# Moving three small pieces of work in a two-layer graph kernel: the x loads, one operand load, and the row degrees

## The chip, the cores and the metric

The kernel runs on one core of a Trainium2 chip. The metric is device time in microseconds (us) of one execution. Engines are named as in the profile: PE is TensorE, DVE is VectorE, ACT is ScalarE, POOL is GpSimd, SP is SyncE, which here only issues DMA transfers.

## The reference: what is computed

The inputs are features x (4096 x 512), an adjacency matrix adj (4096 x 4096, about 0.8% of it non-zero, all entries at or above zero) and a weight matrix W (512 x 512), all fp32.

```python
mask = incidence_m > 0
head = mask / maximum(sqrt(sum(mask * mask, axis=-1)), EPS)
inc = incidence_m + head                      # incidence_m is adj
edge_fea = inc @ cur                          # cur is x
edge_degree = sum(inc, axis=-1)
x = layernorm(x + edge_fea / edge_degree)     # layer 0
A2 = adj + eye
dscale = diagonal(A2) ** -0.5
y = relu((dscale[:, None] * A2 * dscale[None, :]) @ (A2 @ x @ W.T))
x = layernorm(x + y)                          # layer 1
```

The degree of a row is the sum of inc over that row. Since head puts 1/sqrt(count) on each of the count positive entries, the degree also equals the plain row sum of adj plus sqrt(count).

## The kernel before, in words

**Layer 0** multiplies inc (4096 x 4096) by x with one level of a seven-product scheme (Strassen-Winograd): rows and columns are halved, so a block row j (of 16) stands for rows j and j+16 of 128. A block row is cut into four chunks n = 4j + c, each with four inner steps kk of 128. Per kk, `multiply1` issues seven fp32 matmuls into seven PSUM banks; the profile shows each as two instructions. The right operands lie ready in SBUF in `slots[kk]` (seven 256-wide operands, each with two more columns, so W = 258). The two extra columns of B11, B21 and T1 hold ones, so three of the seven matmuls are 258 wide and their column 256 gives the row degree. Block row 0 is done earlier by `multiply_plain`, with four matmuls per kk: first the upper row (h = 0), then the lower (h = 1).

**Where inc comes from.** For every chunk DVE computes raw sums (which POOL sends to DRAM for layer 1), the masks times the row scale (`to_inc`), and the scheme's sums (`add_up`). `prepare1(n + 1)` is written one chunk ahead of `multiply1(n)`. The row scale 1/sqrt(count) of block row j comes from ACT: natural-order tiles `nat` of adj (128 x 512, five buffers, 16 tiles per block row) are loaded on the SP queue; `count(times)` takes each tile, runs Sign in place with a running sum into `cnt` (L377, recorded on L332), and then issues the load of a later tile (L378). `spread(j, 0)` adds the counts on DVE (L384) and takes the square root on ACT (L336). For block rows 1 and 2 the scale then goes through a diagonal matrix `d` on DVE (L393) and a matmul on PE (L408); for later rows through DRAM.

**The start.** SP issues four half chunks of adj (L556), then the loads of x (L315, L316), the other four half chunks, the rest of x, and five `nat` loads. ACT takes signs of the first halves, PE sums them (L343) with some idle products that keep it running (L348), DVE makes the first masks, and the first `multiply_plain` begins. `count(16)` (L594) is written before the last quarter of the upper row, `spread(1, 0)` (L609) after the first quarter of the lower row, and `spread(1, 2)`, with PE's L408, after the second.

**Order.** Every engine takes its instructions in the order in which the program writes them. So what stands behind a waiting instruction on the same engine or on the SP queue waits too. After each block row `combine` empties the seven banks: ACT copies q1 and q5 (L503, L507), DVE adds; PE's next block row needs q1's bank first. These ACT copies stand behind the counts of chunk c = 3. With `deg` (L505, L513) `combine` also collects the degree, and `layer0` divides by it.

**Layer 1** has 224 steps (k, s, p, kk) of seven 512-wide fp32 matmuls. Per step SP loads an operand of adj (`load_up_to`, L217 and others), and every two steps a group of right operands `tr` (`load_b`, L250, three buffers). Group 3 (steps 6 and 7) reads what `operands` leaves for block row 15; that is written at step 1, by POOL. `load_b_up_to` is called at every odd step, at its end (L1026).

Of the kernel before, what the change touches and what calls it, by code (L numbers as in the profile page):

```python
# [8 lines left out]
F32 = mybir.dt.float32  # L9
BF16 = mybir.dt.bfloat16  # L10
AF = mybir.ActivationFunctionType
ALU = mybir.AluOpType

P = 128
# [12 lines left out]
def tile_adj_resnorm_d2(  # L27
# [270 lines left out]
    nc.gpsimd.memset(ones_b, 1.0)  # L298
    ones_f = w1_pool.tile([P, P], F32, name="ones_f", bufs=1)
    nc.gpsimd.memset(ones_f, 1.0)  # L300
    chunks, sums, slots, counts, scale, natural = {}, {}, {}, {}, {}, {}
    xr = {}

    mask = w1_pool.tile([P, 2, CW], F32, name="mask", bufs=1)
# [33 lines left out]
    def count_half(h, c, ps):  # L338

        m = w1_pool.tile([P, 2, CW], F32, name="sr", bufs=2).bitcast(BF16)[:, :, 0:CW]  # L340
        signs(m, chunks[c][:, 2 * h:2 * h + 2, :])
        for z in range(2):
            nc.tensor.matmul(ps, ones_b, m[:, z, :], start=(c + z == 0), stop=(c == NC - 1 and z == 1))  # L343

    def idle_products(times):

# [23 lines left out]
    def count(times):  # L370
        for _ in range(times):
            if not waiting:
                return
            (j, h, t), nat = waiting.pop(0)
            if j not in counts:
                counts[j] = w1_pool.tile([P, 2, NT], F32, name="cnt")
            signs(nat, nat, counts[j][:, h, t:t + 1])  # L377
            load_natural()  # L378

    def spread(j, part):  # L380

        if part == 0:
            n = w1_pool.tile([P, 2], F32, name="n", bufs=2)
            nc.vector.tensor_reduce(n, counts.pop(j), axis=mybir.AxisListType.X, op=ALU.add)  # L384
            to_scale(n, n)
            scale[j] = n
        elif part == 1:
            n = scale.pop(j)
            nc.vector.tensor_scalar(n, n, EPS, None, op0=ALU.max)
            nc.vector.reciprocal(n, n)  # L390
            d = w1_pool.tile([P, 2, P], F32, name="d", bufs=1)
            for h in range(2):
                nc.vector.tensor_scalar(d[:, h, :], ident, n[:, h:h + 1], None, op0=ALU.mult)  # L393
            scale[j] = d
        elif part == 3:

            n = scale.pop(j)
            nc.vector.tensor_scalar(n, n, EPS, None, op0=ALU.max)
            nc.vector.reciprocal(n, n)
            row = dram.tile([P, 2], F32, name=f"sc{j}")  # L400
            nc.gpsimd.dma_start(out=row, in_=n)
            s = w1_pool.tile([P, P, 2], F32, name="sc")
            nc.gpsimd.dma_start(out=s.rearrange("p i h -> p (i h)"), in_=row.rearrange("i h -> (i h)").partition_broadcast(P))
            scale[j] = s.rearrange("p i h -> p h i")
        else:
            d = scale.pop(j)
            ps = spare()
            nc.tensor.matmul(ps[:, 0:2 * P], ones_f, d.rearrange("p h i -> p (h i)"), start=True, stop=True)  # L408
            scale[j] = w1_pool.tile([P, 2, P], F32, name="sc")
            nc.scalar.copy(scale[j].rearrange("p h i -> p (h i)"), ps[:, 0:2 * P])  # L410
# [47 lines left out]
    def multiply1(n, acc, then=None):  # L458
        c = n % NC
        a, s = chunks.pop(n), sums.pop(n)  # L460
        for i in range(CK):
            kk = c * CK + i
            b = slots[kk]
            cols = slice(i * P, (i + 1) * P)
            if then is not None and i == CK - 1:
                then()
            for m, (left, right, w) in enumerate((
                (a[:, A11, cols], B11, W), (a[:, A12, cols], B21, W), (s[:, S2, cols], T2, H),
                (s[:, S1, cols], T1, W), (s[:, S3, cols], T3, H), (s[:, S4, cols], B22, H),
                (a[:, A22, cols], T4, H),  # L470
            )):
                nc.tensor.matmul(acc[m][:, 0:w], left, b[:, right, 0:w], start=(kk == 0), stop=(kk == NP - 1))  # L472

    def multiply_plain(h, c, acc, then={}):

# [12 lines left out]
    def take(h, acc):  # L488

        y = row_tile("z", 2)  # L490
        nc.scalar.copy(y[:, 0:H], acc[0][:, 0:H])
        nc.scalar.copy(y[:, H:D], acc[1][:, 0:H])
        nc.scalar.copy(deg0[:, h:h + 1], acc[0][:, H:H + 1])
        return y

    def combine(acc):

        q1, q2, q6, q5, q7, q3, q4 = acc
        top, low = row_tile("z", 2), row_tile("z", 2)
        p1, p5 = row_tile("p1", 1)[:, 0:W], row_tile("p5", 1)[:, 0:W]  # L500
        u2, u3 = row_tile("u2", 1)[:, 0:H], row_tile("u3", 1)[:, 0:H]
        deg = small.tile([P, 2], F32, name="deg", bufs=2)
        nc.scalar.copy(p1, q1[:, 0:W])  # L503
        nc.vector.tensor_add(top[:, 0:H], q2[:, 0:H], p1[:, 0:H])
        nc.vector.tensor_add(deg[:, 0:1], q2[:, H:H + 1], p1[:, H:H + 1])  # L505
        nc.vector.tensor_add(u2, q6[:, 0:H], p1[:, 0:H])
        nc.scalar.copy(p5, q5[:, 0:W])  # L507
        nc.vector.tensor_add(u3, q7[:, 0:H], u2)
        nc.vector.tensor_add(u2, u2, p5[:, 0:H])
        nc.vector.tensor_add(top[:, H:D], q3[:, 0:H], u2)  # L510
        nc.vector.tensor_sub(low[:, 0:H], q4[:, 0:H], u3)
        nc.vector.scalar_tensor_tensor(low[:, H:D], u3, -1.0, p5[:, 0:H], op0=ALU.mult, op1=ALU.subtract)
        nc.vector.tensor_copy(deg[:, 1:2], p5[:, H:H + 1])  # L513
        return top, low, deg

    def load_rows(j):
        for h in range(2):
# [3 lines left out]

    def layer0(j, C):

        rd = small.tile([P, 2], F32, name="rd", bufs=2)
        nc.vector.reciprocal(rd, C[2])
        stats = []
        for h in range(2):
            y = C[h]
            nc.vector.scalar_tensor_tensor(y, y, rd[:, h:h + 1], xr.pop(h), op0=ALU.mult, op1=ALU.add)
            stats.append(statistics([y]))  # L530
        for h in range(2):
            normalise(C[h], *stats[h])
            nc.gpsimd.dma_start(out=x1_rows[j + h * NP], in_=C[h])

    def operands(j, C):

        top, low, _ = C
        t = row_tile("t", 1, (P, 4, H))
        outer_sums(t, top[:, 0:H], top[:, H:D], low[:, 0:H], low[:, H:D])
        nc.gpsimd.dma_start(out=in_outer(2, j, slice(B11, B11 + 1)), in_=top[:, 0:H].unsqueeze(1))  # L540
        nc.gpsimd.dma_start(out=in_outer(2, j, slice(B21, B22 + 1)), in_=split(low))
        nc.gpsimd.dma_start(out=in_outer(2, j, slice(T1, T4 + 1)), in_=t)
# [7 lines left out]
            work.tile([P, 4, CW], F32, tag="s", name="s")  # L550
    inc11 = work.tile([P, 4, CW], F32, tag="s", name="s")
    scale[0] = w1_pool.tile([P, 2, P], F32, name="sc")
    deg0 = small.tile([P, 2], F32, name="deg", bufs=2)

    def load_half(h, c):
        nc.sync.dma_start(out=chunks[c][:, 2 * h:2 * h + 2, :], in_=adj_q[0, c][:, 2 * h:2 * h + 2, :])  # L556
# [5 lines left out]
    nc.gpsimd.memset(feats[-1][:, 1, T2, 0:H], 1.0)  # L562
    idle = feats[-1][:, 1, T2, 0:H].bitcast(BF16)
    for c in range(NC):
        count_half(0, c, ps)
        idle_products((0, 3, 0, 8)[c])
    for kk in range(10):
        load_x(kk)
    for c in range(NC):
# [2 lines left out]
        load_x(kk)  # L572
    for s in feats:
        nc.gpsimd.memset(s[:, :, B11:B21 + 1, H:W], 1.0)
        nc.gpsimd.memset(s[:, :, T1, H:W], 1.0)
    for _ in range(5):
        load_natural()
    top, low = [bank(0), bank(1)], [bank(6), bank(5)]
# [45 lines left out]
    prepare1(NC)  # L624
    build_last(4)
    multiply_plain(1, 3, low)
    C = top, take(1, low), deg0
    load_rows(0)

    for n in range(NC, NP * NC):  # L630
        j, c = divmod(n, NC)
        if c == 0:
            if j > 1:
                C = combine(acc)
            acc = [bank(m) for m in range(7)]
        if n + 2 >= NP * NC:
            load_up_to(n + 2 - NP * NC)
        else:
            load_chunk(n + 2)
        scales = j < NP - 1 and c == (2 if j == 1 else 1)  # L640
        if scales:
            spread(j + 1, 0)
        if n + 1 < NP * NC:
            prepare1(n + 1, between=(lambda: spread(j + 1, 1 if j == 1 else 3)) if scales else None)
        else:
            prepare(0)
        if n == NC:
            for g in range(5, NP // 2):
                build_last(g)
        multiply1(n, acc, (lambda: spread(j + 1, 2)) if scales and j == 1 else None)  # L650
        count(((6, 6, 4, 6) if j == 1 else (6, 0, 4, 6))[c])
        if j == 1 and c == 1:
            nc.vector.tensor_scalar(dscale, dscale, 1.0, None, op0=ALU.add)
            nc.scalar.activation(dscale, dscale, AF.Sqrt)
            nc.vector.reciprocal(dscale, dscale)
            nc.gpsimd.tensor_scalar(nscale, dscale, -1.0, None, op0=ALU.mult)
        if c == 1:
            layer0(j - 1, C)
        elif c == 2:
            operands(j - 1, C)  # L660
        if c == 3:
            load_rows(j)
# [330 lines left out]
    for n, (k, s, p, kk) in enumerate(steps):  # L993
# [28 lines left out]
                nc.gpsimd.dma_start(out=wt[:, op], in_=parts[f, o])  # L1022
        elif n == 4:
            outer_sums(wt[:, T1:T4 + 1], wt[:, B11], wt[:, T4], wt[:, B21], wt[:, B22])
        if n % 2 == 1:
            load_b_up_to(n // 2 + 3)  # L1026
        for item in items:
            take_up(item)
# [69 lines left out]
```

## Time and profile before

| | |
|---|---|
| median of three runs (lowest to highest) | 2285.16 us (2283.39 to 2285.18) |
| the profiled execution's own time | 2284.03 us |
| its span in the trace | 2282.1 us |
| PE busy | 2255.1 us, 99% of the span |
| DVE, ACT, POOL busy | 1854.4, 417.3, 383.3 us |
| DMA | 555.80 MB, mean 244 GB/s |

The span is what the trace covers; the own time is 1.9 us more. The table of busy time tells which engine is full over the whole; what a change in one place is worth has to be read from the waits and the timeline of that place.

### The profile page before, as it was taken

The numbers are of one execution on the slowest core, as the hardware profiler recorded it, in microseconds if no ns is written. First come the engines' busy times: TensorE is split into PE (matmuls) and PEld (weight loads), VectorE is DVE, ScalarE is ACT, GpSimd is POOL, SyncE is SP. The second block draws the span as 40 slices with busy tenths as digits, with TensorE's granted clock in tenths as the row PEclk, the third lists the DMA queues.
The fourth block names the chain that finished last, engine by engine and source line by source line (L and its number), as shares of the span: only waits on it lengthen the run. The fifth ranks groups of instructions, "written<-read, shape, count | busy, mean of one in ns | idle before, by whom it ended". The sixth has DMA issues, their size and how long they took to land.

```text
span 2282.1 us, 22004 instructions
## 1 busy us (share of the span) xinstructions
PE 2255.1 (99%) x7359; PEld 1380.3 (60%) x7359; DVE 1854.4 (81%) x2619; ACT 417.3 (18%) x991; POOL 383.3 (17%) x548
## 2 busy tenths in 40 slices
PE   8999999999999999999999999999999999999997
PEld 6888888888888844444555444555544444444443
DVE  6988988988988777788876778887666788776788
ACT  4333223332232000000222100122110011100013
POOL 0111112211111110001333300232320000100013
PEclk9999999999999999999999999999999999999999
DMA  9788777878777576575767857576785676766573
GB/s 330 274 287 262 260 233 270 272 262 270 238 240 239 187 266 259 198 283 184 270 240 227 262 209 271 191 283 261 209 256 218 220 258 241 253 238 227 209 269 117
DMA packets 155936, 555.80 MB, mean 244 GB/s; under 512 B 17920, under 2 KB 32272, under 8 KB 117424
## 3 DMA queue, kind: packets, MB, share of 16 engines
q1 hardware_dynamic: 114624, 417.38, 51.6%
q0 software_dynamic: 41200, 137.03, 18.2%
q8 instruction: 58, 0.95, 0.2%
q14 instruction: 54, 0.44, 0.1%
HBM read 434.78 MB, written 119.55 MB: 243 GB/s over the span
## 4 chain that ended last, share of the span: by engine, by line
PE 89%; DVE 5%; DMA 3%; ACT 2%; issue 1%; POOL 0%; SPq 0%; DVEq 0%; ACTq 0%
PE q L278 55%; PE q L472 27%; PE q L766 3%; PE q L485 2%; DMA nat<-adj 2%; DVE s L167 1%; PE q L908 1%; PE q L844 1%; DVE s L169 0%; ACT z L816 0%; ACT nat L332 0%; DVE a L442 0%; DVE mask L435 0%; ACT t L816 0%; DVE ts L257 0%
## 5 line engine op out<-in xcount | busy, mean ns | idle before, releaser
L278 PE MATMUL q<-s,ts 128*128 128x512 f32 x1326 | 612.2, 592 | 0.1
L472 PE MATMUL q<-b,s 128*128 128x256 f32 (+1 forms) x1920 | 454.4, 379 | 0.0
L278 PEld LDWEIGHTS q<-s,ts 128*128 128x128 f32 x1326 | 251.6, 190 | 299.1 <-issue 268.3
L167 DVE TENSOR_TENSOR s<-a 128x1024 f32<-128x1024 f32 x236 | 290.2, 1230 | 161.4 <-PE q L278 131.3
L472 PEld LDWEIGHTS q<-b,s 128*128 128x128 f32 x1920 | 363.1, 189 | 53.1 <-DVE z L510 0.5
L472 PE MATMUL q<-b,a 128*128 128x258 f32 (+1 forms) x1440 | 352.5, 380 | 0.7 <-ACT p L503 0.6
L278 PE MATMUL q<-a,tr 128*128 128x512 f32 x692 | 329.4, 592 | 1.8 <-DMA a<-adj_r 1.8
L472 PEld LDWEIGHTS q<-b,a 128*128 128x128 f32 x1440 | 272.5, 189 | 40.9 <-ACT p L503 1.5
L278 PE MATMUL q<-s,tr 128*128 128x512 f32 x442 | 225.7, 592 | 0.0
L278 PEld LDWEIGHTS q<-a,tr 128*128 128x128 f32 x692 | 129.5, 190 | 145.1 <-issue 138.9
L332 ACT ACTIVATE nat<-nat,tiny 128x512 f32<-128x512 f32 x240 | 170.9, 714 | 235.9 <-DMA nat<-adj 235.7
L278 PE MATMUL q<-a,ts 128*128 128x512 f32 x346 | 176.8, 592 | 0.0
L169 DVE TENSOR_TENSOR s<-a,s 128x512 f32<-128x512 f32 x236 | 167.7, 711 | 8.1
L170 DVE TENSOR_TENSOR s<-a,s 128x512 f32<-128x512 f32 x236 | 167.3, 709 | 8.0
L442 DVE TENSOR_TENSOR a<-a,mask 128x1024 f32<-128x1024 f32 x123 | 150.7, 1225 | 6.6 <-DVE mask L435 0.5
L435 DVE SCALAR_TENSOR_TENSOR mask<-a,sc 128x1024 f32<-128x1024 f32 (+2 forms) x129 | 154.1, 1196 | 2.1
L278 PEld LDWEIGHTS q<-s,tr 128*128 128x128 f32 x442 | 84.0, 190 | 92.1 <-issue 84.6
L684 ACT COPY p<-q 128x512 f32<-128x512 f32 x27 | 15.6, 577 | 631.5 <-PE q L278 631.5
L278 PEld LDWEIGHTS q<-a,ts 128*128 128x128 f32 x346 | 65.7, 190 | 83.0 <-issue 76.1
L425 POOL DMA_DIRECT2D oa<-sr x64 | 57.7, 902 | 283.8 <-DVE sr L416 181.6
L873 POOL DMA_DIRECT2D out<-o x24 | 13.1, 547 | 507.8 <-ACT o L162 507.8
L278 PE MATMUL q<-r,tr 128*128 128x512 f32 x192 | 92.7, 593 | 0.0
(193 smaller groups left out, 2129.4 us busy)
## 6 DMA issues: line engine op xcount, KB each, us to landing
a<-adj_r SPq DMA_DIRECT2D x112, 1024.0 KB, 6.6
a<-oa SPq DMA_DIRECT2D x80, 1024.0 KB, 5.3
nat<-adj SPq DMA_DIRECT2D x240, 256.0 KB, 7.4
a<-adj_q SPq DMA_DIRECT2D x60, 1024.0 KB, 6.2
tr<-ob SPq DMA_DIRECT2D x112, 512.0 KB, 4.0
oa<-sr POOLq DMA_DIRECT2D x64, 512.0 KB, 7.2
oa<-r POOLq DMA_DIRECT2D x32, 1024.0 KB, 9.2
y<-x POOLq DMA_DIRECT2D x64, 256.0 KB, 7.2
```

What stands on the lines that cost most here:

```text
L167: nc.vector.tensor_add(s[:, S3:S1 + 1, :], a[:, A11:A22 + 1, :], a[:, A21, :].unsqueeze(1).to_broadcast([P, 2, w]))
L169: nc.vector.tensor_add(s[:, S2, :], a[:, A11, :], s[:, S1, :])
L170: nc.vector.tensor_add(s[:, S4, :], a[:, A12, :], s[:, S2, :])
L278: nc.tensor.matmul(acc[m], left, right, start=(kk == 0), stop=(kk == NQ - 1))
L332: nc.scalar.activation(y, a, AF.Sign, bias=tiny, scale=2.0 ** 64, accum_out=accum)
L425: nc.gpsimd.dma_start(out=dst, in_=sr.rearrange("p m (k i) -> p (m k) i", i=P))
L435: nc.vector.scalar_tensor_tensor(m, v, 0.0, s.unsqueeze(1).to_broadcast(list(v.shape)), op0=ALU.is_gt, op1=ALU.mult)
L442: nc.vector.tensor_add(z, z, y)
L472: nc.tensor.matmul(acc[m][:, 0:w], left, b[:, right, 0:w], start=(kk == 0), stop=(kk == NP - 1))
L485: nc.tensor.matmul(y[:, 0:w], left, slots[kk][:, op, 0:w], start=(kk == 0 and left is k1), stop=(kk == NP - 1 and left is k2))
L766: nc.tensor.matmul(ps, left[:, e, :], wt[:, right, e, :], start=(e == 0), stop=(e == 1))
L844: nc.tensor.transpose(ps[:, at + i * P:at + (i + 1) * P], C_of[3][h][d // 2][:, 2 * r + d % 2, cols], ident)
```

## The change

Four edits, in this order in time:

1. POOL copies one element of the first sign tile into slot 0 of x, which the first x load then overwrites. So that load, and everything behind it on the SP queue, is issued after ACT has finished the first sign tile.
2. For each `nat` tile ACT first runs a Copy in place with a running sum into a new tile `tot` (L379 of the changed kernel), then the Sign as before. DVE adds these sums per block row and adds sqrt(count), which is the degree. The extra columns go out of `multiply1`, `combine` has no degree work, and POOL no longer writes ones into T1. Block row 0 keeps the 258-wide products.
3. The counts per chunk change from 6, 0, 4, 6 to 5, 4, 5, 2 (block row 1: from 6, 6, 4, 6 to 6, 6, 5, 6); `count(16)` and `count(4)` at the start stay as they are.
4. In layer 1, the call of `load_b_up_to` at step 1 is skipped; step 3 loads groups 3 and 4.

```diff
             if j not in counts:
                 counts[j] = w1_pool.tile([P, 2, NT], F32, name="cnt")
+                totals[j] = w1_pool.tile([P, 2, NT], F32, name="tot")
+            nc.scalar.activation(nat, nat, AF.Copy, accum_out=totals[j][:, h, t:t + 1])
             signs(nat, nat, counts[j][:, h, t:t + 1])
             load_natural()
...
             to_scale(n, n)
+            deg = degrees[j] = w1_pool.tile([P, 2], F32, name="deg", bufs=3)
+            nc.vector.tensor_reduce(deg, totals.pop(j), axis=mybir.AxisListType.X, op=ALU.add)
+            nc.vector.tensor_add(deg, deg, n)
             scale[j] = n
...
-                nc.tensor.matmul(acc[m][:, 0:w], left, b[:, right, 0:w], start=(kk == 0), stop=(kk == NP - 1))
+                nc.tensor.matmul(acc[m][:, 0:H], left, b[:, right, 0:H], start=(kk == 0), stop=(kk == NP - 1))
...
-        nc.vector.tensor_add(deg[:, 0:1], q2[:, H:H + 1], p1[:, H:H + 1])
...
-        nc.vector.tensor_copy(deg[:, 1:2], p5[:, H:H + 1])
...
-        nc.vector.reciprocal(rd, C[2])
+        nc.vector.reciprocal(rd, degrees.pop(j))
...
     for c in range(NC):
-        count_half(0, c, ps)
+        m = count_half(0, c, ps)
+        first_signs = m if c == 0 else first_signs
         idle_products((0, 3, 0, 8)[c])
+    nc.gpsimd.tensor_copy(out=slots[0][:, B11, 0:1], in_=first_signs[:, 0, 0:1])
     for kk in range(10):
         load_x(kk)
...
-        nc.gpsimd.memset(s[:, :, T1, H:W], 1.0)
...
-        count(((6, 6, 4, 6) if j == 1 else (6, 0, 4, 6))[c])
+        count(((6, 6, 5, 6) if j == 1 else (5, 4, 5, 2))[c])
...
-        if n % 2 == 1:
+        if n % 2 == 1 and n > 1:
             load_b_up_to(n // 2 + 3)
```

More of the change, by code (lines that the diff above doesn't have):

```diff
@@ L300, in tile_adj_resnorm_d2 @@
     nc.gpsimd.memset(ones_f, 1.0)
-    chunks, sums, slots, counts, scale, natural = {}, {}, {}, {}, {}, {}
+    chunks, sums, slots, counts, totals, degrees, scale = {}, {}, {}, {}, {}, {}, {}
     xr = {}
@@ L343, in count_half @@
             nc.tensor.matmul(ps, ones_b, m[:, z, :], start=(c + z == 0), stop=(c == NC - 1 and z == 1))
+        return m
     def idle_products(times):
@@ L466, in multiply1 @@
                 then()
[L467 to L470, printed above, removed]
+            for m, (left, right) in enumerate((
+                (a[:, A11, cols], B11), (a[:, A12, cols], B21), (s[:, S2, cols], T2), (s[:, S1, cols], T1),
+                (s[:, S3, cols], T3), (s[:, S4, cols], B22), (a[:, A22, cols], T4),
             )):
-                nc.tensor.matmul(acc[m][:, 0:w], left, b[:, right, 0:w], start=(kk == 0), stop=(kk == NP - 1))
+                nc.tensor.matmul(acc[m][:, 0:H], left, b[:, right, 0:H], start=(kk == 0), stop=(kk == NP - 1))
     def multiply_plain(h, c, acc, then={}):
@@ L492, in take @@
         nc.scalar.copy(y[:, H:D], acc[1][:, 0:H])
-        nc.scalar.copy(deg0[:, h:h + 1], acc[0][:, H:H + 1])
+        nc.scalar.copy(degrees[0][:, h:h + 1], acc[0][:, H:H + 1])
         return y
@@ L499, in combine @@
         top, low = row_tile("z", 2), row_tile("z", 2)
[L500 to L504, printed above, removed]
-        nc.vector.tensor_add(deg[:, 0:1], q2[:, H:H + 1], p1[:, H:H + 1])
-        nc.vector.tensor_add(u2, q6[:, 0:H], p1[:, 0:H])
-        nc.scalar.copy(p5, q5[:, 0:W])
+        p1, p5, u2, u3 = (row_tile(t, 1)[:, 0:H] for t in ("p1", "p5", "u2", "u3"))
+        nc.scalar.copy(p1, q1[:, 0:H])
+        nc.vector.tensor_add(top[:, 0:H], q2[:, 0:H], p1)
+        nc.vector.tensor_add(u2, q6[:, 0:H], p1)
+        nc.scalar.copy(p5, q5[:, 0:H])
         nc.vector.tensor_add(u3, q7[:, 0:H], u2)
-        nc.vector.tensor_add(u2, u2, p5[:, 0:H])
+        nc.vector.tensor_add(u2, u2, p5)
         nc.vector.tensor_add(top[:, H:D], q3[:, 0:H], u2)
         nc.vector.tensor_sub(low[:, 0:H], q4[:, 0:H], u3)
-        nc.vector.scalar_tensor_tensor(low[:, H:D], u3, -1.0, p5[:, 0:H], op0=ALU.mult, op1=ALU.subtract)
-        nc.vector.tensor_copy(deg[:, 1:2], p5[:, H:H + 1])
-        return top, low, deg
+        nc.vector.scalar_tensor_tensor(low[:, H:D], u3, -1.0, p5, op0=ALU.mult, op1=ALU.subtract)
+        return top, low
     def load_rows(j):
@@ L535, in operands @@
     def operands(j, C):
-        top, low, _ = C
+        top, low = C
         t = row_tile("t", 1, (P, 4, H))
@@ L552, in tile_adj_resnorm_d2 @@
     scale[0] = w1_pool.tile([P, 2, P], F32, name="sc")
-    deg0 = small.tile([P, 2], F32, name="deg", bufs=2)
+    degrees[0] = w1_pool.tile([P, 2], F32, name="deg", bufs=3)
     def load_half(h, c):
@@ L626, in tile_adj_resnorm_d2 @@
     multiply_plain(1, 3, low)
-    C = top, take(1, low), deg0
+    C = top, take(1, low)
     load_rows(0)
```

## The prediction

> **What bounds the kernel now.** I read the table of busy time first, then who PE waited for.
>
> ```profile
> PE 2255.1 (99%) x7359; PEld 1380.3 (60%) x7359; DVE 1854.4 (81%) x2619; ACT 417.3 (18%) x991; POOL 383.3 (17%) x548
> ...
> PE q L343 <- ACT sr L332: 6.7, 3, 6.3
> PE q L766 <- ACT p L768: 4.3, 8, 0.9
> PE q L844 <- DVE c L913: 1.8, 1, 1.8
> PE q L278 <- DMA a<-adj_r: 1.8, 1, 1.8
> PE q L472 <- ACT p L503: 0.6, 1, 0.6
> ```
>
> PE is the bound: 27 us of the span are not PE, most of them the start and the tail. So an edit gains only if it shortens PE's own stream or one of these few waits, and loses if it makes a new one. Next, in the timeline, the first place where PE needs something that ACT counts:
>
> ```profile
> 40.88 0.72 ACT L332 ACTIVATE nat<-nat,tiny 128x512 f32<-128x512 f32 x1 [4.83 <-DMA nat<-adj]
> 41.51 0.19 ACT L332 ACTIVATION_READ_ACCUMULATOR nat<-nat,tiny 128x1 f32 x1
> 41.60 0.71 ACT L332 ACTIVATE nat<-nat,tiny 128x512 f32<-128x512 f32 x1
> ...
> 55.95 0.17 DVE L384 TENSOR_REDUCE n<-cnt 128x2 f32<-128x16 f32 x1 [1.40 <-ACT nat L332]
> ...
> 56.40 0.31 ACT L336 ACTIVATE n<-n,half_n 128x2 f32<-128x2 f32 x1
> ...
> 57.15 0.48 DVE L393 TENSOR_SCALAR d<-ident,n 128x128 f32<-128x128 f32 x2
> ...
> 59.01 0.59 PE L408 MATMUL q<-d,ones_f 128*128 128x256 f32 x2
> ```
>
> Sixteen tiles run from 40.88, when the first one lands, to 55.92. DVE is already waiting for them (1.40 us). The diagonal is ready at about 57.6 and PE comes to L408 at 59.01: a margin of only 1.4 us. The end of block row 1 and the start of layer 1:
>
> ```profile
> 121.44 0.72 ACT L332 ACTIVATE nat<-nat,tiny 128x512 f32<-128x512 f32 x1 [4.52 <-DMA nat<-adj]
> 122.07 0.19 ACT L332 ACTIVATION_READ_ACCUMULATOR nat<-nat,tiny 128x1 f32 x1
> 122.16 0.35 ACT L503 COPY p<-q 128x258 f32<-128x258 f32 x1
> ...
> 826.35 0.38 SPq L250 DMA_DIRECT2D tr<-ob  x1
> 826.83 1.04 SPq L217 DMA_DIRECT2D a<-adj_r  x2
> ...
> 832.53 1.02 PE L278 MATMUL q<-a,ts 128*128 128x512 f32 x2
> 835.38 1.98 PE L278 MATMUL q<-a,tr 128*128 128x512 f32 x4 [1.83 <-DMA a<-adj_r]
> ```
>
> At 122 the copy that frees PE's first bank stands behind a late count tile. At 826 the SP queue has stood 16.3 us for block row 15's operands, with the loads of adj behind it, and PE pays at 833.4.
>
> **What the Trainium skill says.** "ScalarE: Activation LUTs", section What ACT_TABLE_LOAD costs: an ACTIVATE on N columns takes 280 ns + 0.833 N with a bias from a pointer, 186 ns + 0.833 N with immediates, and back-to-back ones overlap by 93 ns. Sign (bias `tiny`): 707 ns, and the trace has 714; it agrees. "TensorE: Matmul & The Clock Gate", section What's actually happening: after an idle window of about 3.4 us PE is throttled to half its clock, and needs about as long of work to come back. The trace agrees: the eight idle products from 11.99 run at 0.43 us, the same 128x512 shape at 29.53 at 0.22 us, so 3.6 us of dense work were at half speed.
>
> **The change part by part.**
>
> *256 columns.* 512-wide matmuls follow at 162.58/378 = 0.430 us in the chain, 0.84 ns a column. Three matmuls x 2 instructions x 16 kk x 15 block rows = 1440 instructions lose 2 columns each: 1440 x 1.68 ns = 2.4 us gained. `combine` loses two DVE operations of 0.15 us per row, `spread` gains two of about the same: nothing, and DVE has idle time before each `combine` (21 us of waits for L503, 18 for PE). The second new one waits for ACT's root, some 0.5 us of DVE per row, under the same cover; without it 14 x 0.5 = 7 us. The eight POOL memsets (0.13 us each) were off the path.
>
> *The operand load.* Skipping it at step 1 lets the adj loads of steps 5 and 6 go when their buffers are free, about 815 and 821 instead of 826.8. PE was due at 833.39, started at 835.38, and its next four took 2.06 us instead of 1.72: 2.3 us gained. What is late next: group 3 goes at about 826.4, since its source still lands then, takes 4.0 us (median) and about 1.5 of DVE, ready at 832; PE wants it at step 6, about 837. The step 7 load of adj, now behind both groups, goes at about 827.5, when its buffer comes free anyway, and is wanted at 843. So no new wait.
>
> *x behind the signs.* The fourth half chunk lands at 9.96; the rate fell from 376 to 238 GB/s in the slice from 6 to 7 us, when x was already queued. Without x it would land near 8.3. ACT is then held by its own 1.15 us per tile: four from 5.09 end at 9.7 instead of 11.22; but the three idle products hold PE to about 10.5, and its second pair of sums after that ends near 11.5 instead of 12.15. Gain 0.7 us (0 to 1.5) at PE's start. x itself: issued from 6.6, first data near 8, as before, so no loss. ACT's third sign now also waits for POOL's one-element copy (0.1 to 0.2 us, right after the first sign), long before it needs to. This gain is worth nothing if PE waits later, below.
>
> *Two operations per tile.* Copy has immediates: 0.61 us by the page's price, and no run shows it. Sign works in place on what Copy leaves, so it must wait for the Copy's accumulator read: in the Sign rows that read starts 0.63 and ends 0.82 after the start, so for Copy about 0.53 and 0.72. With 0.02 to 0.03 for the wait, Sign starts 0.74 after Copy, the next Copy 0.71 later: 1.45 us per tile, where it was 0.71. Bounds: 0.52 + 0.71 = 1.23 if nothing waits and they overlap; 1.64 if both take the full 0.82. Sixteen tiles from 40.88: done at 64.2 (60.6 to 67.1). Before, DMA also held them (3.3 us); now reloads have 5.8 us, against 4 to 5.3 measured, and are hidden.
>
> Behind it DVE stands still from 54.5. The first reduce starts at 64.2; the degree reduce (0.1) hides under the root; ACT's three copies and root end 0.75 later; the degree add takes 0.15, and now `build_last` (0.7) comes after that add, where it used to run during the root; then L389 to L393 0.85. The diagonal is ready 2.5 us after the reduce starts, at 66.7 (63.1 to 69.6). PE starts L408 there instead of at 59.01: **7.7 us lost (4.1 to 10.6)**. The start's gain falls into this wait. Everything behind L408 moves along; DVE has 16.1 us of work to the sums of chunk 4, PE 15.2 us to where it wants them, and the cold clock covers the difference.
>
> *Cold clock.* PE then has been idle some 8 us, over the page's 3.4: 3.6 us of work at half speed, 1.8 us lost (0 to 3.4).
>
> *End of block row 1.* After L410 ACT has eleven tiles (were ten) before L503. At 1.45 us, five run until 114.9 (old clock times); the sixth of the last batch is loaded only after the first of that batch, at 116.4, behind a 1 MB chunk that SP can only issue at 115.2. From 6 us (queue alone) to 10 us (the old one took 111.4 to 121.36) it lands at 122.5 to 126.4. Count and copy: PE restarts at 124.3 to 128.2, due at 121.8, and before it lost 0.6. So 1.8 to 5.8 lost, I take 3.7, and 0.5 for a clock gone cold in half of the cases.
>
> *Later rows.* 16 x 1.45 = 23 us of counting in 48.6 us per row; the last batch has only two tiles, loaded a chunk earlier. The wait at 560 (1.0 us, by the same mechanism as at 122) goes.
>
> **Sum** against the profiled execution's 2284.03 (span 2282.1 and 1.9 around it): minus 2.4, 2.3 and 1.0, plus 7.7, 1.8, 3.7 and 0.5, which is +8.0: 2292.0. That execution lies 1.1 below the median; added to the median it is 2293.2. I forecast 2292.5 us, between the two.
>
> **Rivals.**
>
> *The counts stay hidden (faster).* The place is L408, the price is the time per tile: PE comes there at 58.3 with the earlier start, so nothing is lost while 16 tiles take under 14.9 us, 0.93 each. Then only gains remain: 2284.0 - 2.4 - 2.3 - 1.0 - 0.7 = 2277.6 (near 2278.5 from the median). For it: ACT is 18% busy. Against: Sign alone is 0.71, which leaves 0.22 for 512 columns.
>
> *A short wait (within the bound).* Copy overlaps with Sign at 1.23, PE does not go cold, and the tile at 122 lands early: +4.1 + 1.8 - 5.7 = +0.2, with some of the start's stall left 2284.2 to 2288. For it: no trace shows Copy. Against: the dependence in place, and the idle time is over 4 us.
>
> *ACT holds every row (slower).* If each of 14 row ends waits 0.5 us because a tile or the layer norm's roots queue behind counts: +7 on top, 2299.5. Against: half of ACT's time is free.
>
> **How the numbers follow.** Main case 0.68, the short wait 0.18, every row 0.08, hidden 0.06. The likeliest case alone spans 2288 to 2297. The range leaves out the hidden case and the top of the last one: low 2284 from the short wait's end, high 2299. About 0.2% (4.6 us) is what a measurement of this kernel can tell from no change: faster 0.06, same 0.18, slower 0.76.
>
> **What would show it.** DVE's reduce of the counts near 64 after a wait near 10 us; L408 near 66.7 with a PE wait of about 8, PE slow for 3 to 4 us after it; pairs of Copy and Sign at 1.45; a PE wait for the q1 copy at the end of block row 1 and none at later ends; no PE wait for adj at the start of layer 1; 216.6 ns between layer 0's matmuls going to 215. A pair below 1.2 us, a first tile landing 4 us earlier, or waits at every row's end would make the prediction wrong.

## The result, and the profile after

The changed kernel takes 2296.17 us (median of five, 2294.23 to 2297.53), the kernel before 2285.16 us beside it. The ratio is 1.0049 with a 95% interval of 1.0036 to 1.0063: slower. The profiled execution has a span of 2294.3 us, 12.2 more than before. The forecast was 2292.5 in 2284 to 2299.

First the table of busy time, then PE's part of the table of waits (engine, line waited at, whom it waited for: us in total, times, longest), both of the changed kernel:

```profile
PE 2256.3 (98%) x7358; PEld 1383.2 (60%) x7359; DVE 1856.0 (81%) x2619; ACT 585.5 (26%) x1471; POOL 382.5 (17%) x541
```

```profile
PE q L415 <- DVE d L400: 8.5, 1, 8.5
...
PE q L478 <- ACT p L507: 4.2, 1, 4.2
...
PE q L278 <- DVE c L689: 0.5, 1, 0.5
```

ACT has 168 us more to do, and it is still three quarters idle. PE has two new waits, of 8.5 and 4.2 us. They stand at the two places that the prediction named: the diagonal product (L408 before, L415 now) and the first bank after block row 1. The wait of 1.8 us for adj at the start of layer 1 is gone, and so is the one at 560 (0.59 us of waiting, about 1.0 with the slower start behind it).

The first place, in the timeline of the changed kernel (start, duration, engine, line, operation; in brackets the idle time before it and what ended it):

```profile
41.26 0.63 ACT L379 ACTIVATE nat<-nat 128x512 f32<-128x512 f32 x1 [5.60 <-DMA nat<-adj]
41.80 0.19 ACT L379 ACTIVATION_READ_ACCUMULATOR nat<-nat 128x1 f32 x1
...
42.02 0.72 ACT L332 ACTIVATE nat<-nat,tiny 128x512 f32<-128x512 f32 x1
...
42.74 0.61 ACT L379 ACTIVATE nat<-nat 128x512 f32<-128x512 f32 x1
...
64.76 0.17 DVE L387 TENSOR_REDUCE n<-cnt 128x2 f32<-128x16 f32 x1 [10.67 <-ACT nat L332]
...
66.62 0.48 DVE L400 TENSOR_SCALAR d<-ident,n 128x128 f32<-128x128 f32 x2
...
67.25 1.19 PE L415 MATMUL q<-d,ones_f 128*128 128x256 f32 x2 [8.48 <-DVE d L400]
...
68.24 9.65 PE L491 MATMUL q<-b,a 128*128 128x258 f32 x32
```

A pair of Copy and Sign takes 42.74 - 41.26 = 1.48 us here (1.46 as the mean), where one Sign took 0.72. DVE stands still for 10.67 us, then PE for 8.48. The last two lines show the price after the wait: L415 takes 1.19 us, where it took 0.59, and 32 products take 9.65 us. The next 32 are back at 7.10. The busy time by stretch says why. Its columns are start and end, length, then the busy time (and count) of PE, PEld, DVE, ACT and POOL, the clock that PE was granted as a share of full speed, the DMA share and GB/s:

```profile
59.73:63.14 3.41, 0.00 (x0) 0.00 (x0) 0.00 (x0) 3.35 (x10) 0.00 (x0) 1.00 0.60 174
...
69.97:73.38 3.41, 3.41 (x10) 2.67 (x9) 3.38 (x5) 3.35 (x11) 0.00 (x0) 0.50 0.96 359
73.38:76.79 3.41, 3.41 (x17) 3.00 (x16) 3.34 (x5) 1.29 (x4) 1.81 (x3) 1.00 1.03 342
```

PE has no work from 58.8 on. The granted clock falls to half at 63.14 and comes back at 73.38, 6.1 us after PE has started again: 10 products run in the last 3.41 us before that, 17 in the 3.41 us after it. A second stretch at half clock, 138.23 to 141.65, stands behind the end of block row 1. The kernel before has none between 12 us and its tail. The page's row of the clock shows 9 in all forty slices, since a slice is 57 us long. The end of block row 1 in the timeline:

```profile
135.97 0.63 ACT L379 ACTIVATE nat<-nat 128x512 f32<-128x512 f32 x1 [1.64 <-DMA nat<-adj]
...
137.44 0.35 ACT L507 COPY p<-q 128x256 f32<-128x256 f32 x1
...
137.85 1.73 PE L478 MATMUL q<-b,a 128*128 128x256 f32 x4 [4.25 <-ACT p L507]
```

The copy that frees q1's bank stands right behind the pair of a late tile. And layer 1's first loads:

```profile
834.71 0.33 SPq L217 DMA_DIRECT2D a<-adj_r  x1
...
843.59 0.89 SPq L250 DMA_DIRECT2D tr<-ob  x2
...
848.11 0.69 DVE L257 TENSOR_TENSOR ts<-tr 128x512 f32<-128x512 f32 x1 [2.28 <-DMA tr<-ob]
```

The adj load now goes 9 us ahead of group 3. DVE waits 2.28 us for that group, and PE waits for nothing.

### The profile page after: what moved, and what is told of

It reads as the page before. It is cut to its first block, busy times and chain, and to the rows that moved or that the text cites. A ratio compares the mean times of both kernels' runs of the same rounds, so it can differ in the third digit from the quotient of the medians.

```text
span 2294.3 us, 22239 instructions
## 1 busy us (share of the span) xinstructions
PE 2256.3 (98%) x7358; PEld 1383.2 (60%) x7359; DVE 1856.0 (81%) x2619; ACT 585.5 (26%) x1471; POOL 382.5 (17%) x541
## 4 chain that ended last, share of the span: by engine, by line
PE 89%; DVE 4%; ACT 3%; DMA 2%; issue 1%; SPq 0%; POOL 0%; DVEq 0%; ACTq 0%
PE q L278 52%; PE q L478 31%; PE q L770 3%; DMA b<-x 1%; ACT nat L332 1%; DVE s L167 1%; PE q L491 1%; PE q L912 1%; ACT nat L379 1%; DVE s L169 1%; DMA nat<-adj 1%; PE q L848 1%; DVE ts L257 0%; DMA a<-oa 0%; ACT z L820 0%
## 5 line engine op out<-in xcount | busy, mean ns | idle before, releaser
L278 PE MATMUL q<-s,ts 128*128 128x512 f32 x1326 | 612.1, 592 | 0.0
L478 PE MATMUL q<-b,s 128*128 128x256 f32 x1920 | 454.3, 379 | 0.0
L278 PEld LDWEIGHTS q<-s,ts 128*128 128x128 f32 x1326 | 251.7, 190 | 298.6 <-issue 271.2
L478 PE MATMUL q<-b,a 128*128 128x256 f32 x1440 | 350.9, 379 | 4.2 <-ACT p L507 4.2
L278 PE MATMUL q<-a,tr 128*128 128x512 f32 x692 | 329.6, 592 | 0.5 <-DVE c L689 0.5
L278 PE MATMUL q<-s,tr 128*128 128x512 f32 x442 | 225.7, 592 | 0.0
L278 PEld LDWEIGHTS q<-a,tr 128*128 128x128 f32 x692 | 129.5, 190 | 143.8 <-issue 138.2
L278 PE MATMUL q<-a,ts 128*128 128x512 f32 x346 | 176.8, 592 | 0.0
L379 ACT ACTIVATE nat<-nat 128x512 f32<-128x512 f32 x240 | 148.0, 616 | 32.4 <-DMA nat<-adj 32.3
L278 PEld LDWEIGHTS q<-s,tr 128*128 128x128 f32 x442 | 84.0, 190 | 92.1 <-issue 83.9
L278 PEld LDWEIGHTS q<-a,ts 128*128 128x128 f32 x346 | 65.7, 190 | 83.0 <-issue 76.1
```

Source lines behind the costliest of these rows:

```text
L278: nc.tensor.matmul(acc[m], left, right, start=(kk == 0), stop=(kk == NQ - 1))
L379: nc.scalar.activation(nat, nat, AF.Copy, accum_out=totals[j][:, h, t:t + 1])
L478: nc.tensor.matmul(acc[m][:, 0:H], left, b[:, right, 0:H], start=(kk == 0), stop=(kk == NP - 1))
```

## Experiments

The leading theory: ACT's pairs make the diagonal late and hold the end of block row 1. These are two separate losses, each with slow products behind it; the moved operand load and the narrower products are gains. One rival puts the loss down to the hold on x. Another says that the slow products do not come from PE's idle time.

**The two waits apart.** The changed kernel with other counts in block row 1, so that fewer tiles are left before its end:

```diff
-count(((6, 6, 5, 6) if j == 1 else (5, 4, 5, 2))[c])
+count(((8, 6, 5, 4) if j == 1 else (5, 4, 5, 2))[c])
```

> The changed kernel with the counts of block row 1 alone as 8, 6, 5, 4. Theory (two separate losses that add up): the wait of 8.5 us before the L415 product stays, the one at the end of block row 1 goes with its slow clock: 2296.2 - 5.8, about 2290.4 us. Rival (the second wait is a consequence of the first, or is set by the load alone): it stays within 1 us of 4.2 us, 2295 to 2296 us.

Measured: 2288.93 us, ratio 1.0017 (1.001 to 1.0025). In the waits of this kernel the diagonal is as late as in the changed one, and in the timeline the copy of q1 comes 5.7 us sooner:

```profile
PE q L415 <- DVE d L400: 8.4, 1, 8.4
```

```profile
131.78 0.35 ACT L507 COPY p<-q 128x256 f32<-128x256 f32 x1
```

PE no longer waits there. The span falls by 5.9 us (2294.3 to 2288.4), more than the 4.25 us of the wait itself: the rest is the slow stretch behind it, and the second stretch at half clock is gone. The two losses are separate, as the prediction had them.

**Block row 1 with its degrees from PE.** Rows 2 to 15 keep the doubled counting; row 1 gets back the 258-wide products and counts with Sign alone.

```diff
-            nc.scalar.activation(nat, nat, AF.Copy, accum_out=totals[j][:, h, t:t + 1])
+            if j != 1:
+                nc.scalar.activation(nat, nat, AF.Copy, accum_out=totals[j][:, h, t:t + 1])
...
+                w = W if n // NC == 1 and right in (B11, B21, T1) else H
...
+        if row == 1:
+            nc.vector.tensor_add(deg[:, 0:1], q2[:, H:H + 1], w1[:, H:H + 1])
+            nc.vector.tensor_copy(deg[:, 1:2], w5[:, H:H + 1])
```

> The changed kernel, but block row 1 keeps its degree in 258-wide products, and its sixteen tiles get the Sign alone. Theory (sixteen pairs of Copy and Sign ahead of the first diagonal make most of the loss): the PE wait of 8.5 us before the L415 product and the slow 3.1 us behind it go, the wait at the end of block row 1 stays near 4: 2296.2 - 11.6 + 0.2, about 2284.8 us. Rival (ACT's doubled work costs in every row): less than 3 us come back, 2293 us or more.

Measured: 2292.14 us, 1.0032 (1.002 to 1.0045), a partial miss. PE's waits in layer 0:

```profile
PE q L482 <- ACT p L515: 4.5, 1, 4.5
PE q L418 <- DVE d L403: 2.6, 1, 2.6
PE q L482 <- DVE deg L528: 2.0, 1, 2.0
```

The wait at the diagonal fell from 8.5 to 2.6 us, so the pairs made most of it. The end of row 1 still waits 4.5 us, as expected: the tiles counted there belong to block row 3 and have pairs in this run too (L381 in its timeline), so it does not say whether the pairs are needed for that wait. There are two things that I had not expected. The 2.6 us left at the diagonal are one. The third line is the other, a flaw of the edit: I had put the degree add, which reads q2's bank, at the end of `combine`, where it kept that bank from PE. The clock is at half from 129.76 to 140.00 here. With the counts of the run above on top:

```diff
-count(((6, 6, 5, 6) if j == 1 else (5, 4, 5, 2))[c])
+count(((8, 6, 5, 4) if j == 1 else (5, 4, 5, 2))[c])
```

> As the run with block row 1 plain, and the counts of block row 1 go 8, 6, 5, 4 instead of 6, 6, 5, 6, so that fewer tiles stand before the bank copy at its end. Theory: the PE wait of 4.2 us there and the 1.8 us of slow clock behind it go, no other appears: 2284.8 - 5.8, about 2279 us, faster than the kernel before. Rival (the eight tiles only move the wait): a new PE wait at the diagonal of block row 2 or a late layer norm, 2283 us or more.

Measured: 2285.41 us, 1.0002 (0.9994 to 1.001), a miss. Its waits:

```profile
PE q L482 <- DVE deg L528: 2.7, 1, 2.7
PE q L418 <- DVE d L403: 2.6, 1, 2.6
```

The wait for ACT is gone, the flaw has grown, and 2.6 us at the diagonal remain although row 1 counts as before. That pointed to the hold on x.

**The hold alone, the load alone, both.** Three kernels built from the kernel before:

```diff
+    nc.gpsimd.tensor_copy(out=slots[0][:, B11, 0:1], in_=first_signs[:, 0, 0:1])
     for kk in range(10):
         load_x(kk)
...
-        if n % 2 == 1:
+        if n % 2 == 1 and n > 1:
             load_b_up_to(n // 2 + 3)
```

Only the first edit:

> The kernel before with the x loads behind the first signs alone. Theory (the held loads are then issued one by one, the x stream falls below its rate for some 4 us, the nat tiles land later and the margin of 1.4 us at L408 is used up): PE starts 0.4 us or more earlier and waits about 2 us at the diagonal, with some 2 us of slow clock behind it: 2285.5 to 2287.5 us. Rival (the wait at the diagonal of the earlier run was a chance of the DMA): no such wait, 2283.6 us.

Measured: 2285.64 us, 1.0002 (0.9994 to 1.0011). The timeline, of the slowest of its executions (2288.74 us):

```profile
59.41 0.17 DVE L385 TENSOR_REDUCE n<-cnt 128x2 f32<-128x16 f32 x1 [5.40 <-ACT nat L332]
...
61.23 1.19 PE L409 MATMUL q<-d,ones_f 128*128 128x256 f32 x2 [2.53 <-DVE d L394]
...
62.22 8.18 PE L486 MATMUL q<-b,a 128*128 128x258 f32 x32
```

DVE's reduce of the counts comes at 59.41, where it came at 55.95 before, with the same counting. The busy time by stretch shows what is late. Before, after, and with the hold alone:

```profile
8.00:13.00 5.00, 4.57 (x12) 1.20 (x11) 0.69 (x1) 2.32 (x3) 0.00 (x0) 1.00 1.07 365
```

```profile
8.00:13.00 5.00, 4.78 (x11) 1.28 (x10) 0.69 (x1) 2.70 (x3) 0.00 (x0) 1.00 0.97 301
```

```profile
8.00:13.00 5.00, 4.44 (x14) 1.22 (x12) 1.19 (x3) 2.70 (x3) 0.00 (x0) 1.00 0.94 271
```

With the hold the first x load is issued at 6.49 us instead of 2.64; the kernel before has issued six by then. From there they go one after another, 0.65 us apart. The transfers have less to do in these 5 us: (365 - 271) x 5 = 0.47 MB less are moved. The adj halves, the rest of x and the tiles stand behind them. In the four runs with the hold and the Sign alone in row 1, the first tile is taken at 41.57 to 42.30 us and DVE's reduce comes at 59.02 to 59.77; in the three kernels without the hold it is 40.88 to 41.03 and 55.95 to 57.03. The whole margin before L408 was 1.4 us, and all four wait there while none of the three does. So the hold by itself makes the diagonal late. That the lower rate is the way by which it does so fits the order on the SP queue, but no run changed the rate alone.

Only the load of layer 1:

> The kernel before with the later operand load alone. Theory (the run with both moved loads gained 2.3 us at the start of layer 1 and lost it again before L408): no wait for adj at the start of layer 1, nothing else moves: 2284.0 - 2.3, about 2281.7 us. Rival (this load takes as much elsewhere): 2284 us.

Measured: 2282.43 us, 0.9993 (0.9987 to 1.0). PE has no wait for adj. The gain is the 2 us that were expected, at the edge of what can be measured. Both:

> The x loads behind the first signs and the later operand load alone; degrees, widths and counts as before. Theory (the two operations per tile make the loss, the other edits gain): L408 is not waited for, PE starts 0.4 us earlier (15.19 against 15.58), the wait for adj at the start of layer 1 is gone (2.3 us): 2285.2 - 2.7, about 2282.5 us. Rival (the moved loads themselves cost something later): a new PE wait in the first 130 us or near the start of layer 1, 2285 us or more.

Measured: 2285.3 us, 1.0003 (0.9995 to 1.0011), a miss by 2.8 us. The timeline of this kernel at the diagonal:

```profile
60.84 0.67 PE L409 MATMUL q<-d,ones_f 128*128 128x256 f32 x2 [1.97 <-DVE d L394]
61.35 8.79 PE L486 MATMUL q<-b,a 128*128 128x258 f32 x32
69.98 7.10 PE L486 MATMUL q<-b,s 128*128 128x258 f32 x32
```

A wait of 1.97 us and 8.79 - 7.10 = 1.69 us of slow products eat what the load gains. Here too the slow products stand in a stretch at half clock:

```profile
58.19:61.60 3.41, 1.44 (x8) 0.96 (x7) 2.49 (x7) 1.64 (x7) 0.00 (x0) 1.00 0.84 261
61.60:65.02 3.42, 3.42 (x10) 2.69 (x9) 3.38 (x5) 3.15 (x9) 0.89 (x1) 0.50 0.93 333
```

**Keeping PE at work during the wait.** If the slow products come from idle time, work for PE ahead of L415 takes them away, without bringing the diagonal any sooner.

```diff
+    for _ in range(72):
+        nc.tensor.matmul(bank(2)[:, 0:2 * P], ones_b, ones_f.bitcast(BF16), start=True, stop=True)
     spread(1, 2)
```

> The changed kernel with 72 idle bf16 products of 256 columns (about 0.11 us each, 7.8 us in all) on PE just ahead of the L415 product, inside its wait; the wait itself is not shortened. Theory (after the wait PE runs at half clock): the 20 matmuls behind L415 go at 0.217 us from the first, 3.1 us come back: about 2293.1 us. Rival (what follows the wait is slow because operands or DVE are late): the same 3 us are lost, about 2296 us.

Measured: 2315.07 us, 1.0138 (1.0124 to 1.0151). As an experiment it failed:

```profile
59.09 29.26 PE L619 MATMUL q<-ones_f,ones_b 128*128 128x256 bf16 x72
88.15 1.06 PE L415 MATMUL q<-d,ones_f 128*128 128x256 f32 x2
```

The products, each with a bank tile of its own, took 0.406 us apiece, since each waits for the one before, and L415 came 21 us later than in the changed kernel. They did not hold the clock either: they start 0.327 us apart until 63.57, when the clock falls to half, and 0.427 us apart after that. As one accumulation into one tile:

```diff
+    warm = bank(2)
+    for i in range(72):
+        nc.tensor.matmul(warm[:, 0:2 * P], ones_b, ones_f.bitcast(BF16), start=(i == 0), stop=(i == 71))
     spread(1, 2)
```

> The changed kernel with the 72 idle products of 256 columns ahead of the L415 product once more, now as one accumulation into one bank, so that none waits for the one before. Theory (in the earlier run they took 0.406 us each because each waited for the last; after the long wait PE runs at half clock): they take 0.11 us each and end before the diagonal is ready, the wait of 8.5 us shrinks to under 1, L415 comes no later than in the changed kernel, and the 3.1 us behind it come back: about 2293 us. Rival (late operands, not the clock): the same 3 us are lost, 2296 us.

Measured: 2293.99 us, 1.0039 (1.0025 to 1.0053). The timeline:

```profile
58.67 8.02 PE L620 MATMUL q<-ones_f,ones_b 128*128 128x256 bf16 x72
67.31 0.67 PE L415 MATMUL q<-d,ones_f 128*128 128x256 f32 x2 [0.62 <-DVE d L400]
67.81 7.10 PE L491 MATMUL q<-b,a 128*128 128x258 f32 x32
```

The diagonal is as late as in the changed kernel (67.31), but L415 takes 0.67 us instead of 1.19, and the first 32 products 7.10 instead of 9.65: 3.1 us back at this place. The clock now stays at full speed where it was at half in the changed kernel:

```profile
63.14:66.55 3.41, 3.41 (x33) 2.94 (x30) 1.16 (x6) 2.40 (x10) 0.00 (x0) 1.00 0.65 189
```

PE's idle time is the cause of the slow products, by way of the granted clock. The total fell less than that against the runs of before, since the end of row 1 waited 5.0 us in this run, where it was 4.25.

**The pair itself.** Sign works on what Copy leaves. Two runs let them write elsewhere:

```diff
-            nc.scalar.activation(nat, nat, AF.Copy, accum_out=totals[j][:, h, t:t + 1])
+            nc.scalar.activation(junk, nat, AF.Copy, accum_out=totals[j][:, h, t:t + 1])
```

> The changed kernel, but the Copy writes into a scratch tile (bf16, two buffers) instead of in place, so Sign does not have to wait for it; the sums are the same. Theory (the in-place dependence makes a pair 1.46 us): a pair takes 1.32 us (0.61 + 0.71), sixteen take 2.2 us less, L415 comes 2.2 us earlier and the wait at the end of block row 1 is up to 1 us shorter: about 2293.5 us. Rival (the accumulator read, not the dependence, spaces them): a pair stays at 1.46 us and the time at 2296 us.

Measured: 2297.11 us, 1.0059 (1.0045 to 1.0073). The pair is as long as it was:

```profile
41.05 0.63 ACT L380 ACTIVATE junk<-nat 128x512 bf16<-128x512 f32 x1 [5.30 <-DMA nat<-adj]
...
41.81 0.72 ACT L332 ACTIVATE nat<-nat,tiny 128x512 f32<-128x512 f32 x1
...
42.53 0.61 ACT L380 ACTIVATE junk<-nat 128x512 bf16<-128x512 f32 x1
```

The edit did not take the dependence away: Sign still overwrites `nat`, which Copy reads. With the Sign's output moved too:

```diff
-            signs(nat, nat, counts[j][:, h, t:t + 1])
+            signs(junk[:, 1, :], nat, counts[j][:, h, t:t + 1])
```

> The changed kernel, Copy and Sign both writing to scratch (bf16) and only reading the tile, so neither waits for the other. In the earlier run with Copy alone in scratch the Sign still had to wait, since it overwrote what Copy reads. Theory (the wait between the two makes the pair 1.46 us): a pair takes 1.32 us, L415 comes 2.2 us earlier and the end of block row 1 about 1 us: about 2293 us. Rival (the accumulator read spaces them): 1.46 us, 2296 us.

Measured: 2293.86 us, 1.0035 (1.0022 to 1.0047). The timeline:

```profile
41.80 0.63 ACT L380 ACTIVATE junk<-nat 128x512 bf16<-128x512 f32 x1 [6.11 <-DMA nat<-adj]
42.43 0.71 ACT L332 ACTIVATE junk<-nat,tiny 128x512 bf16<-128x512 f32 x1
43.13 0.61 ACT L380 ACTIVATE junk<-nat 128x512 bf16<-128x512 f32 x1
```

Now the pair takes 1.33 us. Over sixteen tiles that should save 2 us, and the wait at the diagonal fell from 8.5 to 7.0, with a first tile 0.5 us later. The dependence is worth 0.13 us of the pair; the second operation is worth the rest.

**A version without the losses.** Row 1 with its degrees from PE and the counts 8, 6, 5, 4; the degree add moved up, so that q2's bank comes free at once; x not held; the load of layer 1 moved.

```diff
         nc.vector.tensor_add(top[:, 0:H], q2[:, 0:H], p1)
+        if row == 1:
+            nc.vector.tensor_add(deg[:, 0:1], q2[:, H:H + 1], w1[:, H:H + 1])
...
-    nc.gpsimd.tensor_copy(out=slots[0][:, B11, 0:1], in_=first_signs[:, 0, 0:1])
```

> Block row 1 with 258-wide products and the Sign alone, its degree added right behind the first sum as in the kernel before; later rows by Copy and 256 wide; counts of block row 1 as 8, 6, 5, 4; the later operand load; x loads as before. Theory (each loss was in block row 1 or in the held x loads): no PE wait over 1 us before the end of layer 0: 2284.0 - 2.3 (adj) - 2.3 (columns) - 1.8 (both old row-end waits), about 2277.6 us. Rival (ACT's doubled counting costs in later rows too): 2282 us or more.

Measured: 2278.76 us, ratio 0.998 (0.9971 to 0.9989) against the kernel before. It beats both kernels. Its waits (with `spread`'s product now at L418) and its timeline:

```profile
PE q L783 <- ACT p L785: 4.3, 8, 0.7
...
PE q L482 <- DVE s L169: 0.6, 1, 0.6
```

```profile
59.12 0.59 PE L418 MATMUL q<-d,ones_f 128*128 128x256 f32 x2
59.55 7.10 PE L495 MATMUL q<-b,a 128*128 128x258 f32 x32
```

PE walks through the diagonal without a wait, and ACT still does the doubled counting of the fourteen later rows (574.2 us busy). So that counting costs nothing where 48 us per row cover it. Against the run with its two waits of 2.6 and 2.7 us, the span is 8.0 us shorter (2284.2 to 2276.2); the waits and slow products of those two places come to about 8.9.

## Why the prediction was right, and where it was off

The direction, the two places and the mechanism were right. The terms, in the order of the prediction's sum, against what the spacing of PE's instructions and the waits show:

| term | predicted | measured |
|---|---|---|
| 256 columns | -2.4 | about -2.5 |
| wait for adj, start of layer 1 | -2.3 | -2.4 |
| wait at 560 | -1.0 | -1.1 |
| L408 (now L415) later | +7.7 | +8.2 |
| slow products after it, L415 itself too | +1.8 | +3.2 |
| end of row 1 | +3.7 | +3.7 (4.25 less 0.6 before) |
| slow products after it | +0.5 | +1.8 |
| new small waits in layer 1 | 0 | about +1.7 |

L408's term is its start, 67.25 instead of 59.01; PE's own start came 0.39 us earlier (15.19 instead of 15.58, predicted 0.7), which the wait swallowed. The right column comes to +12.6; the span grew by 12.2. The predicted sum was +8.0: short by a third, mostly in the slow products (2.7 us) and the small waits (1.7). The result lies in the range because the range was 15 us wide.

- *256 columns*: in the chain of waits, 40.07 us for 185 products before are 216.6 ns each, and 40.15 for 186 after are 215.9:

```profile
149.97 40.07 PE q L472 x185
```

```profile
149.94 40.15 PE q L478 x186
```

  3360 instructions in fifteen rows, by 0.7 ns each, are the predicted 2.4.
- *Two operations per tile*: predicted 1.45 us, measured 1.46. That Sign waits for the Copy and its accumulator read was the right reading: the run without that dependence has 1.33. "ScalarE: Activation LUTs" of the Trainium skill, section What ACT_TABLE_LOAD costs, gave 0.61 for the Copy, and the groups of the changed kernel give 616 ns.
- *L408*: 7.7 predicted; the first tile landed at 41.26 instead of 40.88, and DVE's reduce came at 64.76 instead of 64.2. The term is short by about 0.5.
- *x itself: no loss*. This step failed. The prediction looked at when the first x arrives and not at what the queue behind it then does. The six loads that went out during the first signs are missing, the stream falls from 365 to 271-301 GB/s, and what stands behind, the count tiles too, is later. The hold alone made a wait of 2.53 us and gained nothing at the end. In the changed kernel the pairs take longer than the late tiles, so of this only the later first tile (0.38 us) shows in the total.
- *Cold clock*: the mechanism was right (half the clock was granted, and the accumulation of 72 products took the slowness away), the size was half. The prediction took 3.6 us of work at half speed; it was 6.1 (67.25 to 73.38), and the 32 products lost 2.55 us and L415 another 0.6. Its reading of the eight idle products from 11.99 was wrong: the clock was already granted in full from 11.90 on. They are 0.432 us apart because each waits for the one before, as in the run with 72 separate products. So the start of the kernel gave no measure of the slow stretch. At the end of row 1 I gave it half a chance; it came, and cost 1.8.
- *End of block row 1*: right in place and size. With eight tiles in the first chunk, and so nine behind the diagonal, the wait is gone although every tile there has its pair. How the 4.25 us divide between the eleventh tile and the pairs stays open: every run with eleven tiles has pairs there, and with ten single counts, in the run with the hold alone, the same copy made PE wait 1.0 us.
- *Operand load*: PE's wait went, as predicted. Group 3 was expected at 826.4 and is issued at 843.59. About 13 us of that is the shift of all that PE does by then; the other 4 are its source, which landed late: the SP queue stands 8.4 us for it. DVE waited 2.28 us, and PE's cover held. The margin was smaller than I said.
- *Layer 1's small waits*: 0.5 us at L278 for L689 and 0.9 more at the projections (5.2 against 4.3 in total). No term had them. The last version has 4.3 at the projections again. What makes them was not tried.

## What to carry to other kernels

An engine that is 18% busy over the whole can be the bound of one stage: ask how many us of its work stand between the arrival of the data and the instruction that needs it, and double that before adding an operation per tile. A wait of the bounding engine can cost more than its length, since the first work after it can run slow (3.1 us here after 8.48); the granted clock, read in stretches of a few us, shows it. And a load that is held back is late together with all that is queued behind it, so a margin of 1.4 us some 50 us later can be lost to it.

## What the runs showed of the hardware

- The clock goes down after waits of PE that are shorter than I thought: after 1.97 us in the run with both moved loads (1.69 us lost) and 2.53 us with the hold alone (1.08, and 0.6 in the diagonal product). "TensorE: Matmul & The Clock Gate" of the Trainium skill, section What's actually happening, speaks of an idle window of about 3.4 us. The length agrees with these traces, but PE need not be idle for all of it; there the measurement decides.
- The length of a wait alone does not set it. In all thirteen traces the clock changes on a grid of 3.41 us steps: the stretches at half clock last 3.41, 6.83, 10.24 and once 27.31 us, leaving out the tail. By the busy time of PE in each step between 12 and 2260 us, every step with 1.97 us or more of idle time was followed by half clock (15 of them), and every one with up to 1.67 us by full clock, but for the products that waited for each other. The wait of 1.83 us at 835 in the kernel before lies across an edge, at 834.51: 0.95 us of it falls in each step, and the clock stays at 1.00. It was followed by only 0.34 us of slowness.
- Coming back took a step in which PE was nearly always busy: the clock returned after steps with at most 0.32 us idle, and not after one with 0.70 us (66.55 to 69.97 in the changed kernel). So 8.48 us of waiting gave 10.24 us at half clock.
- Small bf16 products of 256 columns started 0.327 us apart at full clock when each had a bank tile of its own, and 0.11 us apart (8.02/72) as one accumulation. Of the two, only the accumulation held the clock.
- On ACT a second operation that overwrites what the first reads waits just as one that reads what the first wrote: 1.46 to 1.48 us per pair for both, 1.33 without either.
